# Another split of a second layer between two ways of computing its experts, a longer pause behind each scatter, and a new order of the instruction streams

## The chip, the cores and the metric

The kernel runs on one core of one Trainium2 chip. The metric is the device time of one execution in microseconds. Before the change the median of three runs is 879.16 us (878.42 to 881.28).

## The reference

Two layers over x of shape (8, 512, 128): causal attention and a mixture of experts, then an RWKV block and the same mixture of experts again, each with a layer norm ahead of it and a residual. The mixture has 32 experts; each token goes to its best four, with at most 4·4096·4/32 = 2048 pairs for an expert, and a shared expert is added.

```python
x = L0_attn_a_embeddings                                  # (8, 512, 128)
x = x + attention(_layernorm(x), W_Q, W_K, W_V)
x = x + _L0_ffn_ref(_layernorm(x), Wg, W1, W2, W3, Ws1, Ws2, Ws3)
x = x + rwkv(_layernorm(x), ...)
x = x + _L0_ffn_ref(_layernorm(x), Wg, W1, W2, W3, Ws1, Ws2, Ws3)
# _L0_ffn_ref, over the tokens xf (4096, 128):
scores = jax.nn.softmax(xf @ Wg, axis=-1)
weights, indices = jax.lax.top_k(scores, TOP_K)           # TOP_K = 4
...
for e in range(E):                                        # E = 32, H = 64
    pos = jnp.nonzero(pair_expert == e, size=C, fill_value=P)[0]
    ...
    out = swiglu(xf[tok], W1[e], W2[e], W3[e]) * w[:, None]
    y = y.at[tok].add(out)
z = swiglu(xf, Ws1, Ws2, Ws3)
return (y + z).reshape(B, S, D)
```

## The kernel before

A sequence is a block of 512 tokens by 128 channels, kept in SBUF in a tile `res` of its own through both layers; everything is float32. Eight sequences, numbered 0 to 7, pass both layers.

The mixture of experts can be computed in two ways, and a table, `RUNS`, says for each layer which sequences take which.

- *By all experts* (`FULL`): `full_up` multiplies the whole sequence with the first matrices of two experts at a time (16 pairs, line 706: two matmuls of 128x512 for each), forms the gated hidden values (lines 709 to 714, one activation and three VectorE operations of 128x512), and `full_down` adds the second matrices' products up in PSUM (line 676, four matmuls of 128x128 for each pair). The gates come from `gates`, which writes them to HBM; `full_up` loads them back spread over the partitions (line 695, tile `g`, two buffers).
- *Through pages* (`PAGED`): two or three neighbouring sequences form a group. `route` works out for every token and each of its four experts a row in a paged table in HBM. `scatter` (line 505) writes the normalized tokens there by 16 indirect DMAs for a sequence, issued by POOL, with a pause behind each: a clear of a small tile, `idle` (line 307), that nobody reads. `experts` goes through the group's pages, four pages of 128 rows to a unit: a load (tile `xg`), then stages turned (transposes, L345 and L563), up (L575 to L589), down (L596, L601) and give (L608, L614), and a store to `ys`. `combine` (line 656) adds the results to `res` by 16 indirect gathers with addition, again issued by POOL. A group of n sequences has `pages_of(n)` pages, which is n·512·4/128 + 31, made up to a multiple of four.

Before the change layer 1 has sequences 0 and 7 by all experts and the groups 1 to 3 and 4 to 6; layer 2 has the groups 0 to 2 and 3 to 5, and sequences 6 and 7 by all experts. A group of three has 80 pages, so 20 units.

The order is written out by hand, or by a program outside of the file. The work is split into streams, Python generators that emit a few instructions and yield. The string `ORDER` names a stream by two characters for each step, and `play` steps the streams in that order. On each engine the instructions then stand in exactly that order and are executed in it, each waiting for what it needs; so an instruction that waits holds up all behind it on its engine. SP issues the plain loads and stores in the same way. The streams' letters are: `a` attention and routing of layer 1, `s` scatter, `x` shared expert, `d` and `e` the two halves of a sequence by all experts, `k l m n` the four stages of a group's units, `u` combine; `r` the RWKV block and the routing of layer 2, and `t`, `y`, `D`, `E`, `K L M N`, `v` for layer 2 what `s`, `x`, `d`, `e`, `k l m n`, `u` are for layer 1. The digit is the sequence, or the group for k to n.

Two things on POOL beside scatters and gathers matter: the inverse roots of the norms (lines 334 and 819) are computed there, and they stand in the same queue. Two PSUM buffers of two banks (`ps2`) are shared by the up stage of the pages and by `full_up`.

Of the kernel before, what the change touches and what calls it, by code (L numbers as in the profile page):

```python
# [79 lines left out]


ORDER = (
    "a1a2a2a0a1a2a2a1a0a3z0a2a1a0a6a3z0a1a2a3a4a2a1a0a1a6a6a4a0a2a2a5a1z0a1a2a2a0a4a5a1a1a2a5a2a1a1a2"
    "a0a3a1a3a2a7a2a1a2a1a2a1a1a0a2a7a2a3a1a1a6a2a0a1a3a2a7a2a1a2a1a2a1a0a2a2a3a1a2a4a0a1a1a3a2a1a2a0"
    "a2a0a2a1a0a0a2a2a3a1a5a2a0a3a2a2a1a1a0a2a3a2a1a7a2a1a2a0a3a6a6a2a1a6a2a6a0a2a0a3a6a0a1a2a0a2a1a2"
    "a1a1a3a6a1a0a3a1a0a3a6a0a6a3a0a0a1a0a6a1a1a3a3a6a3a0a1a3a1a0a1a0a0a6a1a1a3a6a3a3a6a6a0a0a3a6a3a0"
    "a6a0a3a0a3a6a0a3a0a3a6a0a3a0a6a4a6a6a4a0a3a3a6a6a0a0a3a4a6a3a0a6a0a3a0a3a0a3a0a4a6a4a6a0a3a4a3a6"
    "a0a0a3a2a1a0a3a2a3a3a1a1a2a3a1a3a2a4a4a4a2a1a3a5a5a5a1a5a2s1a5a5a5a7a5a5a7a0a2a7a2a7a0a3s2a0x2a6"
    "x2a3a4x2a4a5x2a3a3d0a5a6s2a4d0a4x2d0x2a3a4x2a5a5x0s2a3a6a5x0a3a6l0l0a4l0a6a5a4a6a5d0a6s3a6d0a6d0"
    "x3a4x3a4a5a4a5x3a6a4a5d0a4a5s3a5x3a6a4d0a5x3d0x0a4d0a5x3s3a4x0x3a5a4d0a5x0a4a5a4x0a5s3a4x0a4a4a5"  # L90
    "a4a7a4a5a5a7a4a5s2a7a4a4a5a6a4a5a4x1e0a5a6a7a5a6a4x1a4s1a6x1a5a7a4e0a5x1e0d0a7e0d0a7a4a4a5a4x1s1"
    "d0a4a5a4d0a7x1a7a4d0x1s1d0a4a4d0a7e0a4e0a6d0d0a4d0k0a6a5e0a5a4x4a5a5d0s4x4d0a5d0k0a5e0k0k0l0k0d0"
    "a5s4l0l0l0l0a5m0a5e0m0d0l0l0l0d0s4m0a5m0k0k0k0l0k0d0n0a5s4d0n0l0l0a5l0d0x5e0x5d0m0m0l0x5s5d0l0l0"
    "l0d0k0d0e0k0k0m0k0l0m0x4x5l0l0a7n0s5l0l0n0k0x5x5k0l0l0l0m0x5a6m0s5k0l0a6a6k0m0n0x4l0l0l0n0e0m0k0"
    "a6s5l0k0m0n0a7n0m0n0l0l0x4d0l0a6n0d0k0a6m0k0n0l1s6m0d0l1l0n0n0l0l0l0l0n0k0l0l0l1m0k0l0e0m0n0s6k0"
    "a7l0n0k0m0a7l0n0l0l0x4m0n0k0l0x4k0s6m0l0l0n0l0m0a7x6n0k0a7l0x6k0x6m0l0l0n0l0m0a7s6l0n0a7k0l0l0m0"
    "l0n0k0m0a7k0n0l0a7k0m0n0a7l0l0a7l0m0x6l0n0a7x6k0l0l0m0l0n0k0m0a7n0k0a7l0k0k0l0l0m0l0n0k0m0a7l0n0"
    "a7k0l0l0m0l0n0k0m0x6k1n0a7l0x6m0l0l0n0l0m0a7l0n0a7k1l0l0m0l0n0k1m0a7n0k1a7l1k1a7m0n0m0l1l1d0a7l1"
    "n0d0k1m1d0k1n0l1n0m1a7e0l1l1l1l1a7k1m1l1n1m1u2a7k1d0l1l1d0n1n1d0a7m1k1m1a7k1l1n1d0l1l1l1a7d0k1u2"
    "m1d0k1n1m1e0n1l1a7d0d0l1l1d0n1e0n1u2l1l1e0k1l1l1m1l1k1m1k1m1a7e0m1r0k1l1a7a7n1l1l1r0l1l1a7n1k1m1"  # L100
    "r0u2r0l1n1a7a7m1r0r0r0k1l1l1u1n1a7k1r0m1r0k1r2m1l1r0r0r0l1l1d7l1k1m1r0r0l1m1r2r0d7l1r0r0u1k1r0n1"
    "r2r0r0x7l1r2r0r0r2r0d7r0u1n1n1n1n1x7r0n1r0r0l1r0k1m1r2d7u1m1r2k1r0l1r2r2l1l1x7l1l1r2r2m1k1m1l1r2"
    "r0k1l1r0u3r0l1l1k1m1l1r0r1m1n1k1d7l1r0l1r2x7r0d7m1r0n1m1r1r2k1r2l1r0d7u3k1r0r2d7r0l1r1r2r0l1l1r1"
    "n1k1m1x7r0r0k1r1r1x7u3r0r0r1r0r2r0r1r2r2r2d7u3r2n1m1r2x7l1r0r0l1l1l1r2m1r0k1r1r0k1n1r1r0r1r1r3n1"
    "m1l1r1r0r1r3r0n1l1r2e7r0l1e7r0l1r0r1n1n1r0m1k1n1r0n1m1k1k1l1r1r0r1n1k1l1l1l1r1k1r0n1m1r0r1e7m1l1"
    "n1r0n1k1n1r0l1r1l1r0y0y0l1t0m1r1m1n1r1l1r1n1l1l1l1t0m1r1m1n1r1l1n1l1l1l1t0m1r1m1r1r3r3r2r2d7r1t0"
    "d7r2r1d7r3e7r3r2n1r3n1d7r1r3r3r2r1r1y0r2d7u4r3r3r1r2r3r1r2r1r1r3d7r3e7r1r2d7r1u4r3d7r1r1r2r3r2d7"
# [5 lines left out]
    "r4r3d7r4r5r6e7r4r5r4r3t1y2y2r4r4r3r6r6r6y2y2r5r3r6e7r5t1r5r7r3r5r3r5r3r6r6y2r5r5r6r7r3r5r6r7t1r7"
    "r5r3r3r6r5r4r3r6r5r4r4r3r7K0r4r5r5r5r5K0K0K0K0L0r3r4r4y3r5t3L0r5r6L0L0y3r6y3r6r6M0K0M0t4L0r5K0N0"
    "r6L0r7y3N0r5y3L0L0r6r6M0K0t4r5L0M0r5N0K0y3N0L0r6L0L0L0y3r7t4L0L0L0M0K0r7r6r7M0r6K0N0r7r6M0N0K0t4"
    "L0M0K0r6N0y4N0L0L0L0L0y4K0M0L0L0L0M0N0K0r5r6M0N0K0t3L0M0r5r7N0K0L0L0y4r6N0L0r5K0M0L0M0N0K0t3L0L0"
    "r5N0L0L0r5K0r6M0L0K0r5r6M0r7L0L0r5N0r6r7L0N0r5t3M0K0M0y4K0N0L0L0r6r7r5r6L0N0y4M0L0M0N0r5r5r7K0N0"
    "r6K0y4L0L0L0r7L0y4r5M0K0M0N0K0N0L0L0L0L0r5K0M0L0L0L0M0N0K0r5M0N0L0L1t5M0r6r7L1N0L1L0L0K0r6r6N0K0"
    "L0r7L0r6M0L0L0K0L0t5M0r6N0K0r6M0L0N0K0L0M0r6N0L0L0K0L0N0t5r6M0L0K0r6M0N0L0L0K0K0N0L0K0M0L0L0K0L0"
    "y5M0N0t5K0L0r6N0M0L0r6M0N0L0L0L0r6r6N0L0L0L0r7y5K1r7M0r6r6M0r7r7N0r7r6M0N0K1M0r6N0K1L1N0r6r7K1K1"  # L120
    "L1L1r6L1L1r6K1M1L1v0r7r6M1L1N1K1L1L1N1r6K1M1L1L1L1K1r6M1K1M1r6r7L1K1M1N1L1L1r6v0r7N1L1L1r7N1L1L1"
    "M1L1N1K1M1M1K1r6r7M1v0y5L1r6r6N1L1L1L1K1r6N1N1K1L1N1r6M1L1L1K1L1r6M1N1K1L1r6v0N1M1L1L1K1L1y6M1N1"
    "K1L1y6N1y6M1L1L1K1L1y6M1D6N1K1M1y6L1N1M1r7K1L1L1N1L1v2K1L1N1M1r7L1L1K1L1y6M1K1r7M1L1v0N1M1L1K1L1"
    "D6L1N1v2K1N1y6D6M1N1K1D6r7M1y5K1L1r7y5N1L1L1r7D6N1L1D6r7v2D6M1K1r7L1M1N1K1L1L1L1L1N1r7L1L1L1M1K1"
    "M1y5v2K1r7L1y5M1L1L1N1L1M1K1N1N1K1M1L1M1N1N1L1L1L1K1N1D6v1K1D6M1K1D6M1r7v2K1L1r7N1L1L1K1L1L1N1K1"
    "r7L1L1L1M1v1r7r7E6M1M1N1M1L1N1N1r7L1D6L1L1N1r7v1M1r7r7M1N1r7r7v1E6N1E6D6E6D6D6D6D6D6D6r7E6D6D6v4"
    "D6v1D6D6E6r7r7E6E6r7D6D6r7v4r7r7D6r7D6E6D6D6D6D6D6D6v4r7D6D6r7r7r7r7E6E6D6D6D6D6v4r7D6D6r7y7E6y7"
# [15 lines left out]
def kernel(ctx: ExitStack, tc: tile.TileContext, x, small, vecs, w13, w2, out):  # L143
    nc = tc.nc
# [158 lines left out]
    idle = const.tile([P, PAUSE], F32, tag="idle", name="idle")  # L303

    def pause():

        nc.gpsimd.memset(idle, 0.0)  # L307
# [190 lines left out]
    def scatter(f, b):  # L498

        _, xn, _, rows = routed[f][b]  # L500
        _, lo, _, g = run_of(f, b)
        key = f"scatter{f}_{g}"
        for j in range(NJ):
            for k in range(TOPK):
                i = nc.gpsimd.indirect_dma_start(  # L505
                    out=xs[g][:, :],
                    out_offset=bass.IndirectOffsetOnAxis(ap=rows[:, j, k : k + 1], axis=0),
                    in_=xn[:, j, :],
                    in_offset=None,
                    bounds_check=DUMP + P - 1,  # L510
                    oob_is_err=False,
                )
# [504 lines left out]
```

## Time and profile before

| | us |
|---|---|
| median of the timed runs | 879.16 |
| profiled execution | 944.87 |
| span of the profiled execution | 943.2 |
| scatters on POOL, 192, one | 1.004 |
| clears on POOL, 192, one | 0.279 |
| gathers on POOL, 192, one | 1.612 |
| first and last scatter of layer 1 | 99.3 and 271.4 |
| gathers of layer 1 | 315 to 563 |
| gathers of layer 2 | 747 to 938 |

The profile is of one execution, and its span is longer than the timed runs. An engine's busy time is the time in which at least one of its instructions was under way. Rows of groups name line, engine, operation, what is written and read, and the count; then busy time in us and mean duration in ns of one; then the idle time of the engine just ahead of them. A matmul of float32 appears as two records. For POOL's indirect DMAs the slice is POOL's own part.

### The profile page before, as it was taken

What the parts mean: (1) busy time and instruction counts of PE and PEld (TensorE: products, weight loads), DVE (VectorE), ACT (ScalarE), POOL (GpSimd) and SP (SyncE); (2) the same over time, 40 slices, a digit from 0 to 9 for tenths busy, and PEclk for the clock granted to TensorE, in tenths of its full rate; (3) what the DMA queues carried; (4) which work ended last, traced back from release to release, by engine and by line L of the source; (5) the groups of instructions that cost most, each with busy time, mean ns of one, the idle gap of its engine ahead of it and who ended that gap; (6) DMA issues with size and microseconds to landing.
All of it is one profiled execution on the core that took longest, in us unless ns stands there. A gap on an engine that the chain in (4) does not pass through costs nothing.

```text
span 943.2 us, 14326 instructions
## 1 busy us (share of the span) xinstructions
PE 783.6 (83%) x4096; PEld 550.8 (58%) x4096; DVE 588.5 (62%) x2008; ACT 475.0 (50%) x1130; POOL 615.3 (65%) x682
## 2 busy tenths in 40 slices
PE   4878678958869987896999978887996999999953
...
POOL 6100676768350588864888888968534387888776
PEclk9989979979979999998999979788997999999987
...
GB/s 279 242 220 129 99 68 35 127 104 100 133 92 155 140 136 154 85 78 87 95 34 74 34 34 43 34 89 111 141 130 85 134 176 243 158 108 120 142 86 53
DMA packets 159275, 108.15 MB, mean 115 GB/s; under 512 B 18144, under 2 KB 147552, under 8 KB 158944
## 3 DMA queue, kind: packets, MB, share of 16 engines
...
## 4 chain that ended last, share of the span: by engine, by line
POOL 26%; PE 19%; issue 17%; DVE 4%; ACT 3%; DMA 1%; another core or an unknown queue 1%; POOLq 1%; DVEq 0%; ACTq 0%
POOL res L656 21%; PE o L608 4%; PE acl L575 3%; POOL xs L505 3%; PE turn_x L345 2%; PE ac L706 1%; PE kk L929 1%; POOL rstd_p L819 1%; PE acl L596 1%; PE kv L938 1%; DMA xg<-xs 1%; POOL idle L307 1%; PE s L524 1%; DVE h L586 1%
## 5 line engine op out<-in xcount | busy, mean ns | idle before, releaser
L656 POOL DMA_INDIRECT res<-ys,rows x192 | 309.4, 1612 | 75.7 <-issue 53.3
L505 POOL DMA_INDIRECT xs<-xn,rows x192 | 192.8, 1004 | 104.5 <-issue 38.4
L706 PE MATMUL ac<-fT,pair 128*128 128x512 f32 x256 | 124.8, 617 | 17.2 <-DVE g L713 9.6
L608 PE MATMUL o<-w2s,hz 128*128 x640 | 93.4, 290 | 16.0 <-ACT hz L601 7.5
L575 PE MATMUL acl<-w13s,xgTs 128*128 x640 | 95.3, 295 | 12.4 <-issue 5.6
L608 PEld LDWEIGHTS o<-w2s,hz 128*128 128x128 f32 x640 | 84.2, 201 | 30.0 <-issue 11.4
L575 PEld LDWEIGHTS acl<-w13s,xgTs 128*128 128x128 f32 x640 | 86.0, 206 | 24.5 <-issue 13.0
L334 POOL TENSOR_TENSOR rstd_f<-rstd_f,nhalf 128x4 f32<-128x4 f32 x16 | 19.4, 1213 | 121.3 <-DVE rstd_f L332 59.1
L709 ACT ACTIVATE fh<-ac 128x512 f32<-128x512 f32 x64 | 38.1, 596 | 103.8 <-PE ac L706 69.2
L706 PEld LDWEIGHTS ac<-fT,pair 128*128 128x128 f32 x256 | 47.1, 198 | 62.2 <-issue 39.5
L676 PEld LDWEIGHTS fsum<-w2s,fh 128*128 128x128 f32 x512 | 64.1, 195 | 16.8 <-issue 12.8
L601 ACT COPY hz<-acl 64x256 f32<-64x256 f32 x160 | 58.4, 365 | 28.2 <-PE acl L596 17.3
L676 PE MATMUL fsum<-w2s,fh 128*128 128x128 f32 x512 | 65.9, 278 | 2.1 <-DVE fh L714 2.1
L586 DVE SCALAR_TENSOR_TENSOR h<-h,acl 128x256 f32<-128x256 f32 x80 | 33.6, 420 | 53.0 <-ACT h L583 44.3
L712 DVE SCALAR_TENSOR_TENSOR fh<-fh,ac 128x512 f32<-128x512 f32 x64 | 43.8, 684 | 35.0 <-ACT fh L709 34.1
L614 ACT COPY oc<-o 128x512 f32<-128x512 f32 x80 | 46.7, 585 | 37.0 <-issue 13.3
L580 DVE TENSOR_TENSOR wt<-acl,xg 128x4 f32<-128x4 f32 x80 | 12.8, 160 | 80.7 <-PE acl L575 36.9
L563 ACT COPY xgTs<-turn_x 128x512 f32<-128x512 f32 x80 | 46.8, 585 | 24.5 <-PE turn_x L345 10.4
L345 PE MATMUL turn_x<-ident,xg 128*128 128x128 f32 x320 | 51.6, 287 | 5.8 <-ACT xgTs L563 2.7
L583 ACT ACTIVATE h<-acl 128x256 f32<-128x256 f32 x80 | 30.7, 384 | 47.1 <-DVE wt L580 35.5
L307 POOL MEMSET idle<- 128x192 f32 x192 | 53.5, 279 | 0.1
L713 DVE TENSOR_TENSOR g<-g,ac 128x512 f32<-128x512 f32 x64 | 43.5, 680 | 10.1 <-DMA g<-gd 10.1
...
## 6 DMA issues: line engine op xcount, KB each, us to landing
...
xs<-xn,rows POOLq DMA_INDIRECT x192
res<-ys,rows POOLq DMA_INDIRECT x192
...
```

The source lines that it names most:

```text
L307: nc.gpsimd.memset(idle, 0.0)
L345: nc.tensor.transpose(p[:, j * P : (j + 1) * P], src[:, j, :P], ident)
L505: i = nc.gpsimd.indirect_dma_start(out=xs[g][:, :], out_offset=bass.IndirectOffsetOnAxis(ap=rows[:, j, k : k + 1], axis=0), in_=xn[:, j, : ...
L563: nc.scalar.copy(xT, p)
L575: nc.tensor.matmul(acl[:, j, :EW], xT[:, j * P : (j + 1) * P], w13f[:, bass.ds(at[j], EW)], start=True, stop=True)
L601: nc.scalar.copy(z[half, i, :].rearrange("p (j c) -> p j c", c=H), hT[half])
L608: nc.tensor.matmul(o[:, j * P : (j + 1) * P], z[:, j % 2, j // 2 * P : (j // 2 + 1) * P], w2h[j % 2][:, bass.ds(at[j], P)], start=True, st ...
L614: nc.scalar.copy(flat(oc), o)
L656: nc.gpsimd.indirect_dma_start(out=xa[:, j, :], out_offset=None, in_=ys[g][:, :], in_offset=bass.IndirectOffsetOnAxis(ap=rows[:, j, k : k ...
L676: nc.tensor.matmul(p[:, j * P : (j + 1) * P], h[:, j * P : (j + 1) * P], w, start=False, stop=stop and j == NJ - 1)
L706: nc.tensor.matmul(ac[:, s, :], pair[:, i, s, :], xT, start=True, stop=True)
L712: nc.vector.scalar_tensor_tensor(h, h, 1.0, ac[:, 0, :], ALU.add, ALU.mult)
```

## The change

Three things. In layer 2, sequence 3 is computed by all experts, and the second group has sequences 4 and 5 alone; the first group stays. The pause behind each scatter, in both layers, is two clears in place of one. `ORDER` is new as a whole: it has the streams of the new split (`D3` and `E3` come, `t3` and `v3` go, the second group's streams are shorter), and all others stand in another order too.

```diff
@@ -34,7 +34,7 @@
 PAGED, FULL = True, False
 RUNS = (
     ((FULL, 0, 1), (PAGED, 1, 4), (PAGED, 4, 7), (FULL, 7, 8),),
-    ((PAGED, 0, 3), (PAGED, 3, 6), (FULL, 6, 8),),
+    ((PAGED, 0, 3), (FULL, 3, 4), (PAGED, 4, 6), (FULL, 6, 8),),
 )
@@ -80,54 +80,54 @@
 ORDER = (
-    "a1a2a2a0a1a2a2a1a0a3z0a2a1a0a6a3z0a1a2a3a4a2a1a0a1a6a6a4a0a2a2a5a1z0a1a2a2a0a4a5a1a1a2a5a2a1a1a2"
...
-    "r4r4r5r5r2r4u6r2r4r5r2r5r2r5r5r3r2r3r4u6r5r4r2d7r4d7r5r2L0r3r4L0r3d7r5r4r4r4r5t2L0r5r5r4d7r4r5r5"
...
-    "D7D7D7D7E7E7D7v5D7E7v3D7D7D7D7D7E7D7D7v5D7D7D7E7E7D7D7D7D7E7D7D7v5D7D7D7E7E7D7D7D7D7E7D7v5E7E7E7"
-    "v5"
+    "a2a0a2a0z0a2a2a2a2a2z0a1a0a6a1a3a0a6a1a2a3a2a0a2a0a7a7a1a3a2a2a2a2a2a0a1a6a7a0a1a5a0a0a0a2a1a2a0"
...
+    "r4t1r4r5r3r4r6r4r7r5r5r5r3L0r5r5r5r5r3r6r5r4r4r4y2r5r5r6y2D3D3t2r5r4r4D3y3y3r4r5y3r4y3r5y3r7r6r7"
+    "r7r6r6r5r6y3r5r5D3D3y3D3D3E3r7r7D3D3t2t2E3E3r6L0t2t4r5D3D3D3D3r6r6r5r5r6r5r6E3E3r5D3D3y4D3D3r6y4"
...
+    "D3r5r5r5D3E3D3r5r5t1t1t1K0r5D3K0K0r6r5D3E3K0D3D3r5t4D3L0L0t4L0E3K0r5r6r5L0K0r6r5M0D3E3M0r5r7r6r6"
...
+    "E6v5D7D7D7E7D7D7D7E7E7D7D7D7D7D7E7D7D7D7E7D7D7D7D7E7E7v5D7D7D7D7E7D7E7D7D7D7E7D7D7D7D7D7E7D7D7E7"
+    "D7D7D7D7D7D7D7E7D7D7D7E7v4E7v4E7E7v4v4v4"
 )
@@ -304,7 +304,8 @@
     def pause():
 
-        nc.gpsimd.memset(idle, 0.0)
+        for _ in range(2):
+            nc.gpsimd.memset(idle, 0.0)
```

The functions that the new streams call, `full_up`, `full_down`, `gates` and `experts`, are unchanged.

More of the change, by code (lines that the diff above doesn't have):

```diff
@@ L82 @@
 ORDER = (
-    "a1a2a2a0a1a2a2a1a0a3z0a2a1a0a6a3z0a1a2a3a4a2a1a0a1a6a6a4a0a2a2a5a1z0a1a2a2a0a4a5a1a1a2a5a2a1a1a2"
[L84 to L107, printed above, removed]
@@ L108 @@
-    "r1r3r3r1d7r3d7r1r1r3r2u4d7r2r1r3r1r2r3r3r3r2e7r2r1u4r1r3r3r2r1r1r3r2r2r3d7d7r2r1r1r2d7u5r3r1r4r1"
-    "r2r2r1d7r4r1r2d7r1r2r3e7u5r4r1e7r4e7y0d7r4r3r1d7r3r4d7y0r2r3e7r1r1u5d7r4r1y0r4r1r3r2r4d7r2r1y1r4"
-    "r4d7u5y1r3d7r4y0y1d7y1r4r3r4r4r2r4r4d7r3u6r4y1r4y1r4r2d7r4r3y1r2r3r3r4r4e7r3r3r2e7r4r3u6r3r4r3r3"
-    "r4r4r5r5r2r4u6r2r4r5r2r5r2r5r5r3r2r3r4u6r5r4r2d7r4d7r5r2L0r3r4L0r3d7r5r4r4r4r5t2L0r5r5r4d7r4r5r5"
-    "d7r4r6t2r4r5d7e7r4r4d7r5d7r4r5r4d7r5t2e7d7r4r4r5r5r5d7r4t2d7r5r4r5r5e7r4r4e7r3y2r5r6y2r4r5t1r5r4"
@@ L113 @@
[L113 to L127, printed above, removed]
@@ L128 @@
-    "y7y7D6D6D6D7v3E6y7y7D6D6D6y7v4E7E6E6D6D6E6v3D7D7D7D7D7E6D7D7E6D7v3D7D7E7E7D7D7E7D7D7v3D7D7D7E7D7"
-    "D7D7D7D7E7E7D7v5D7E7v3D7D7D7D7D7E7D7D7v5D7D7D7E7E7D7D7D7D7E7D7D7v5D7D7D7E7E7D7D7D7D7E7D7v5E7E7E7"
-    "v5"
+    "a2a0a2a0z0a2a2a2a2a2z0a1a0a6a1a3a0a6a1a2a3a2a0a2a0a7a7a1a3a2a2a2a2a2a0a1a6a7a0a1a5a0a0a0a2a1a2a0"
+    "a2a0a2a5a3a0a0a2a3a0a3a5a0a2a1a1a2a4a1a4a0a0a0a2a1a2a0a2a2a2a6a0a3a1a0a1a0a0a2a2a3a2a2a0a0a1a0a2"
+    "a1a2a2a0a1a4a1a0a3a2a0a2a1a1a3a3a3a2a2a1a0a1a0a3a3a5a2a2a1a0z0a1a1a0a6a6a1a0a6a1a3a2a2a0a0a3a3a1"
@@ new lines @@
+    "a0a1a6a5a1a2a2a3a1a1a0a0a3a0a6a6a1a0a0a1a1a3a0a0a0a1a1a1a0a1a5a3a3a0a4a2a1a2a1a3a3a1a0a2a0a0a3a4"
+    "a1a1a2a3a6a1a0a1a3a1a4a1a1a6a5a2a0a1a5a0a0a6a6a1a6a3a6a6a3d0a1a1a4a4a3a7a2a3a7a1a6a6a2a7a1a6a4a4"
+    "a1a6a2a5a5a5a6a5a4a6a6a4a7a7a2a2a3s1a4a3a2a6a3a3d0d0a6a6a5a4a3a3a3s2a6a5a3a4a4a3a6a4a6a6a3a4a4a4"
+    "x2a4a5x2a3s1s1a3a6a5a5x2a4s2a6a6a3a6d0a4d0a3a4a3a5a5a5x2a6a6a6a3a3a5x2a4x0a5a3x0x0a4a4a3a3a5a7a4"
+    "a4a4a5a7a7a5a4a3a3a7a4a4a4a4a5x0x0d0d0d0a3d0a5a7a7a4a4a4x0x0a5a4e0a4a4d0a7a7a5e0a5a7a7e0a5a5a5a5"
@@ new lines @@
+    "d0d0a7a5a3a7s1a7a4a4a6a5a7a5s2s2a5a4e0x1a5a6d0a6a6a5x1a4e0d0a7a4l0x1d0a5a7l0l0a4d0a4a7x2d0x2d0a4"
+    "e0a6d0d0d0d0a7d0a6a6d0a6a7e0a6a7a4a7d0a7e0a7e0s3a4x3a4d0x3a4a7d0d0a6x3d0x3e0a7a4x3a4d0x3a7s3s3s3"
+    "d0x3a6x4a5e0x1a7x4d0d0x1d0d0a7a7x4d0k0x1s4s4a7s4d0x4s4a5x4x1a5a5a5a5a5k0k0k0k0a5l0l0l0l0l0a5l0m0"
+    "l0l0a5m0k0e0m0k0k0n0m0k0n0e0a5a5n0n0l0l0l0l0l0l0l0a6m0m0l0k0a6a6a6a5k0k0m0m0d0l0d0a7a7a6x4x4a6d0"
+    "l0n0n0l0n0l0d0s6e0a7m0d0k0k0n0d0m0k0n0a7l0d0l0l0l0d0a5k0s6n0d0m0m0x5l0l0a7d0x5k0l0a7l0x5x5m0n0m0"
@@ new lines @@
+    "k0d0n0x5k0e0l0d0s6a7l0l0a7l0l0e0l0l0l0k0k0m0m0e0n0l1m0m0k0k0l0a7l0l0l0e0n0l0n0l0l0k0k0s6l0r0m0m0"
+    "n0r0a7n0n0x6l0l0m0k0l0l0m0k0n0n0n0m0a7k0l0m0l0x6r0a7k0l0r0l0k0m0l0s5n0a7a7a7x6l0r0r0l0x6s5m0k0x6"
+    "x6a7l0x6r0s5r0l0l0l0m0m0k0k0r0r0r0l0r0k0r0l0r0r0r0r0r0l0l0n0m0n0n0n0k0r0r0a7n0l0m0k0k0r0m0a7r0k0"
+    "l0m0r0l0n0l0n0n0n0n0l0l0l0l0l1m0m0l0k0s5k0n0l1k0m0m0r0l0l0l0l0n0n0l0l0l0l0k1x7d7x7x7m0x7m0n0m0m0"
+    "n0r0x7n0n0n0k1k1r0k1l1l1r0l1r0l1r0m1d7m1n1r0k1r0d7n1d7d7k1r0r0r0r0l1k1d7r0l1l1u2r0l1r0r0r0m1d7k1"
@@ new lines @@
+    "m1k1d7l1d7d7l1r0l1r0n1r0l1l1k1m1l1l1n1m1k1l1r0r0r0u2r0m1m1l1l1u2l1u2k1k1l1r0k1r0m1r0l1x7k1m1l1r0"
+    "l1l1l1x7u1l1l1l1k1r0n1n1m1n1e7m1k1k1n1n1e7r2m1r0m1d7d7d7k1r0l1r0r0l1l1e7l1n1l1r0e7l1m1l1n1m1k1n1"
+    "d7l1d7r2r2m1r2r0r0m1k1k1l1k1r0r2d7r2r0l1n1r0d7l1l1n1d7r0r0r2k1m1n1m1d7l1n1k1l1l1u1u1l1r2r2r2r2l1"
+    "l1l1k1m1k1n1n1n1m1l1k1m1u1n1m1r2t0r2r2r2r2r2r1l1l1e7n1l1l1n1n1e7k1r2r1y0m1n1t0r2r2k1m1d7e7d7r2r1"
+    "r2y0l1t0n1y0r1r1r1d7l1l1d7r2l1k1d7d7r1n1r1k1m1r1r2m1u3r1l1l1l1l1k1r1r1k1m1r2l1n1r1l1m1k1l1l1l1l1"
@@ new lines @@
+    "n1e7l1e7k1k1l1m1k1r1r2n1m1l1n1y0k1l1m1l1k1n1r1l1m1r1r1l1m1n1k1l1n1l1r2r1l1m1y0r1r1n1r1r1r2m1l1r1"
+    "r1n1r1l1m1n1u3n1n1x5r1x5d7d7l1u3d7u3y0l1r2t0r1y0r1d7d7r1m1m1r3d7e7n1n1d7d7d7d7d7e7r3r3r2d7d7r3d7"
+    "r2r1e7r1r3r3d7e7d7d7d7r3r1r3r2r3r1r3r3r3r2r1e7r3r3u4r3e7r3r2r3r3r3u4r1r3r1r1r1r1r1r1r1r3r3r2r2r1"
+    "r2r3r1r1r3r3u4r3r2d7r2r2d7r2r2r2d7d7u4d7d7r3r3r3r2r4r1r2u6r1r1r1e7r4r1r2r4r3r1r4r3r3r2e7r4r2r2r1"
+    "u5r3r4r4e7r3r1r4r4r2r7r3r1r4r4r1r2r2r4r4r4r4r1r1r4r4r4r4r1r3r3r3r3r3r4r4r4r3r3r3u6r4r3u5u6r3r3r3"
@@ new lines @@
+    "r3r2r3r2r4r2r4r1r3r1r2r2r4r2r4u6r4r4r4r1r3r2r4r4r1r4r3r4r1r1y1y1y1r4y1r3r4y1r3u5r4u5r4r3r2r3r6r2"
+    "r7r4r3r4r2y1r4r7r5r6r4y1r4r4r4r4r2r4r4r7r7r5r2r4r7r5r3r4r5y2y2y2r4y2r3r6r5r7r3r5r4r3r3r4r5r5L0y2"
+    "r4t1r4r5r3r4r6r4r7r5r5r5r3L0r5r5r5r5r3r6r5r4r4r4y2r5r5r6y2D3D3t2r5r4r4D3y3y3r4r5y3r4y3r5y3r7r6r7"
+    "r7r6r6r5r6y3r5r5D3D3y3D3D3E3r7r7D3D3t2t2E3E3r6L0t2t4r5D3D3D3D3r6r6r5r5r6r5r6E3E3r5D3D3y4D3D3r6y4"
+    "y4r5D3D3E3r5D3D3r5r5y4r6y4y4r6r7r6y4r5r5r6r5r5r5D3D3E3D3D3r6r5E3r5r6r5r5r6r7E3r6r6r5r5D3D3D3r7D3"
```

12 lines of the change are left out of this document (added).

## The prediction

> **What bounds the kernel now.** I read the page first (shares and slices), then busy time by stretch, cut at the ends of the expert groups, then POOL's timeline, then the group rows for prices.
>
> ```profile
> PE 783.6 (83%) x4096; PEld 550.8 (58%) x4096; DVE 588.5 (62%) x2008; ACT 475.0 (50%) x1130; POOL 615.3 (65%) x682
> ...
> PE   4878678958869987896999978887996999999953
> ...
> POOL 6100676768350588864888888968534387888776
> PEclk9989979979979999998999979788997999999987
> ```
>
> TensorE is the busiest engine, yet it has 160 us of idle time in 943.2, and nowhere one long hole: no single engine is the bound throughout. The stretches show who is:
>
> ```profile
> 0.00:99.00 99.00, 73.18 (x364) 49.78 (x364) 54.08 (x300) 55.70 (x146) 23.44 (x78) 0.95 0.89 207
> 99.00:186.00 87.00, 70.54 (x328) 45.93 (x329) 55.40 (x237) 31.77 (x78) 66.06 (x103) 0.90 0.34 87
> 186.00:312.00 126.00, 97.75 (x630) 80.30 (x629) 63.36 (x214) 56.62 (x150) 59.05 (x93) 0.89 0.44 118
> 312.00:461.00 149.00, 126.46 (x693) 92.11 (x692) 109.62 (x345) 90.81 (x218) 111.31 (x88) 0.93 0.50 106
> 461.00:625.00 164.00, 145.63 (x549) 83.53 (x548) 123.67 (x416) 89.25 (x183) 135.64 (x124) 0.93 0.29 54
> 625.00:744.00 119.00, 100.53 (x576) 77.34 (x575) 69.70 (x225) 68.66 (x166) 63.93 (x98) 0.90 0.41 111
> 744.00:832.00 88.00, 83.72 (x566) 66.99 (x565) 50.75 (x166) 59.42 (x152) 70.80 (x46) 1.00 0.84 177
> 832.00:943.00 111.00, 85.80 (x403) 54.87 (x401) 61.89 (x112) 22.81 (x42) 85.09 (x54) 0.90 0.58 106
> ```
>
> Columns: window, length, busy PE, PEld, DVE, ACT, POOL, clock, DMA share, GB/s. I call A the first four rows (layer 1, 461 us), B 461 to 625 (from the end of layer 1's experts to the start of layer 2's), C 625 to 744 (layer 2's first group), D 744 to 832 (second group), E the tail. POOL paces B: its gathers and scatters follow each other without a hole:
>
> ```profile
> 561.88 1.56 POOL L656 DMA_INDIRECT res<-ys,rows  x1 [0.30 <-issue]
> 563.74 1.07 POOL L505 DMA_INDIRECT xs<-xn,rows  x1 [0.30 <-issue]
> 564.81 0.27 POOL L307 MEMSET idle<- 128x192 f32 x1
> 565.26 1.48 POOL L505 DMA_INDIRECT xs<-xn,rows  x1 [0.18 <-issue]
> 567.18 0.98 POOL L505 DMA_INDIRECT xs<-xn,rows  x1 [0.17 <-issue]
> ```
>
> A gather comes every 1.86 us (558.14, 560.02, 561.88 in that timeline), an undisturbed scatter every 1.41 us. POOL also ends the kernel: the chain that ended last is gathers from 749 to 938 us, while TensorE's last matmul ends at 929.
>
> ```profile
> L656 POOL DMA_INDIRECT res<-ys,rows x192 | 309.4, 1612 | 75.7 <-issue 53.3
> L505 POOL DMA_INDIRECT xs<-xn,rows x192 | 192.8, 1004 | 104.5 <-issue 38.4
> L706 PE MATMUL ac<-fT,pair 128*128 128x512 f32 x256 | 124.8, 617 | 17.2 <-DVE g L713 9.6
> L676 PE MATMUL fsum<-w2s,fh 128*128 128x128 f32 x512 | 65.9, 278 | 2.1 <-DVE fh L714 2.1
> L307 POOL MEMSET idle<- 128x192 f32 x192 | 53.5, 279 | 0.1
> ```
>
> **What the Trainium skill says.** "TensorE: Matmul & The Clock Gate", part 1 on the clock gate: after about one idle window of 3.4 us the clock is halved. The trace agrees: granted clock 1.00 in D, where PE is 95% busy, 0.89 to 0.90 where it is 78 to 84% busy. So filling PE's holes pays twice. "Perfetto Trace Analysis", section on the software-generated DMA of GPSIMD: POOL's slice is the making of descriptors, not the transfer; a clear behind it therefore adds to POOL's time and cannot overlap it, as the timeline shows. "SBUF — State Buffer", on who interferes with whom: a GpSimd operation and some VectorE operations exclude each other on a shared port. Here no sign of it: L586 takes 421 ns under scatters, 419 under clears and 420 with POOL idle, so a second clear should cost POOL alone.
>
> **The change part by part.** Sequence 3 of layer 2 leaves the pages. The group of three (80 pages, 20 units) becomes a group of two: 2·512·4/128 + 31 = 63, so 64 pages, 16 units. One unit costs PE (95.3 + 93.4 + 51.6 + 32.9)/80 = 3.42 us, DVE 1.58 and ACT 2.48 from the rows of its lines; four units are 13.7, 6.3 and 9.9. A sequence by all experts costs PE (124.8 + 65.9)/4 = 47.7, DVE 131.7/4 = 32.9, ACT 38.1/4 = 9.5. Net: PE +34.0, DVE +26.6, ACT about 0. All PE rows add to 899 us where the engine is busy 783.6, so +34 is some +30 of busy time.
>
> POOL loses 16 gathers (16 × 1.86 = 29.8) and 16 scatters with their clear (16 × 1.45 = 23.2), and gains a clear behind each of 176 (176 × 0.279 = 49.1): −4 in all. But the clears are paid early, in A and B (148 of the 176 scatters stand there) and the gathers are saved in the tail. On SP, 8 page loads and stores go and 8 gate loads, 1 gate store come; with a DMA share of 0.29 in B I cost them at nothing (bounds −2 and +3: what hides them is that idle queue; a load in front of a page load would add its landing).
>
> The new order. I count, from the order of instructions on each engine, what stands between the same landmarks, each at its row's duration. PE rows, before and after: A 418.9 and 437.3, B 159.4 and 198.1, C 118.0 and 119.3, D 106.2 and 104.1, E 96.8 and 76.1. Gathers and scatters on POOL in B: 48 and 32, then 48 and 36; in D and E 48 and 48 gathers before, 48 and 32 after.
>
> A: the first group's 48 scatters take 99.3 to 178.9 us, 67.7 of issue and 12 of waiting for routing (POOL runs in order; behind each wait stand scatters, and behind these the first page load). Second clears add 13.4, of which the 12 of waits can absorb most. The second group's 13.4 hide: it ends at 272, its loads start at 303. PE has 18.4 more in rows, 16 busy, beside 93 idle. Bounds 0 and +22; I take +10, half of the PE work hidden.
>
> B: PE work is 198.1 × 145.6/159.4 = 181 us. POOL: 4 scatters more (6.8), 32 second clears (8.9), two more roots (2.4): 164 + 18 = 182. Both must fit; at D's 95% PE needs 190, at B's own 89% 203. Sequence 3's matmuls stand in this stretch and in C. Bounds 182 and 203; I take 192, +28.
>
> C: same work (101.6 busy against 100.5), better filled, since sequence 3's matmuls spread over it: bounds −12 and +4, I take −2. D: −1.
>
> E: POOL no longer ends it. Its 32 gathers are 59.5, with some 7 left over from D and 5 for the last store 72. PE: 76.1 × 85.8/96.8 = 67.5 busy, at 97% 70, plus the stall which the last sequence has today on its gate load, 9.6 (below), plus 6 for the copy and store: 85, −26. Bounds −32 and −18.
>
> ```profile
> DVE g L713 <- DMA g<-gd: 10.1, 1, 10.1
> ```
>
> Sum: 10 + 28 − 2 − 1 − 26 = +9, a span of 952. The profiled execution took 944.87 us for a span of 943.2; the median of the timed runs is 879.16, 0.932 of that span. 952 × 0.932 = 888.
>
> **The rivals.** *The filler is free.* Sequence 3 fills the trough of 550 to 750 us, where windows of 50 us have PE at 80 to 89% and the slices' clock falls to 0.7, while the tail still shrinks: A 0, B +20, C −10, D 0, E −28, so −18 and 862 us. For it: the shortest stretches of PE idle are spread exactly there, and the clock is won back. Against: B asks PE, DVE and POOL together for over nine tenths. It decides from the point where A, B and C together grow by less than 27 us. *POOL blocks in order.* The new order puts a normalization root of sequence 6 in front of the whole scatter of sequence 3 in layer 1, and one of sequence 5 before the last 12 scatters of the first group in layer 2; if DVE reaches them late, experts start late: A +22, B +39, C +4, E −26, so +39 and 915 us. For it: POOL waited 34.3 us for one such root before (at 273 us, with nothing due behind it); here scatters are due. *It cancels.* A +5, B +22, C −2, D 0, E −26 gives −1, 878. That the change doesn't do what it says is excluded by the order: 352 clears, 176 scatters, 76 units.
>
> **How the numbers follow.** Forecast (slower by about 1%) 0.40, free filler 0.36, blocked POOL 0.15, cancelling 0.09. The forecast's own range is 882 to 900; the other cases lie on both sides, so that for 8 in 10 I go from 860, just below the free filler's sum, to 912, just short of the blocked POOL's. A measurement of this kernel tells about 0.3% from no change: faster 0.36, same 0.09, slower 0.55.
>
> **What would show it.** Right: end of layer 1's experts near 471, layer 2's first page transposes near 663, N-group ends near 780 and 866, PE working until some 6 us before the end and POOL idle before it; clears 352 × 0.28; PE busy near 814. Wrong: layer 2's experts start before 650 (filler free, clock above 0.93), or after 675 with a long POOL wait on a root (blocked). A tail longer than 95 us would mean that the end is not PE's.

## The result and the profile after

| | us |
|---|---|
| kernel after, median of 4 runs | 888.11 (886.71 to 889.83) |
| kernel before, 4 runs beside it | 878.79 (876.61 to 881.28) |
| ratio | 1.0106, 95% interval 1.0071 to 1.0141 |
| profiled execution of after, its span | 886.87, 885.2 |

The change makes the kernel about 1% slower. The first lines of its page, the busy times and the slices:

```profile
PE 778.0 (88%) x4206; PEld 542.3 (61%) x4206; DVE 607.6 (69%) x2017; ACT 471.2 (53%) x1124; POOL 615.0 (69%) x810
...
PE   3999887989978899898798859969999999999993
...
POOL 6214777777774687877888887677736527888776
PEclk9999998979989999999799969989999999999997
```

A slice is 22.1 us. TensorE's row has its weak places where POOL scatters: the fifth to seventh digit (8, 8, 7: 88 to 155 us) beside layer 1's first group, the twentieth to twenty-seventh (down to 5 and 6: 420 to 597 us) beside layer 2's.

The execution from which the prediction was worked out (span 943.2) was not like the timed ones: the kernel before, profiled again as it was (run before_again below), has a span of 875.3, and the extra 68 us stand in A (45) and C (23). From here on this second profile stands for before, unless the first is named. Its stretches, cut at the same landmarks (first scatter, first transposes of the first group's pages, end of the first group, end of the second, then for layer 2 first transposes, end of the first group, end of the second); columns as in the prediction: window, length, busy PE, PEld, DVE, ACT, POOL, clock, DMA share, GB/s:

```profile
0.00:99.00 99.00, 73.19 (x365) 50.19 (x365) 54.58 (x301) 56.14 (x146) 23.69 (x79) 0.95 0.86 207
99.00:178.00 79.00, 68.06 (x328) 43.75 (x329) 54.46 (x234) 31.09 (x77) 66.31 (x102) 0.96 0.37 96
178.00:261.00 83.00, 78.97 (x579) 66.99 (x576) 57.66 (x194) 51.19 (x137) 58.01 (x94) 1.00 0.59 163
261.00:419.00 158.00, 134.57 (x751) 98.71 (x750) 116.04 (x370) 97.17 (x234) 111.85 (x89) 0.95 0.52 112
419.00:581.00 162.00, 143.69 (x544) 82.76 (x543) 122.57 (x413) 88.14 (x182) 135.27 (x123) 0.93 0.29 52
581.00:679.00 98.00, 93.07 (x587) 73.01 (x585) 70.96 (x228) 68.35 (x168) 64.59 (x99) 0.97 0.51 139
679.00:769.00 90.00, 85.97 (x568) 68.37 (x569) 50.48 (x165) 59.03 (x150) 73.05 (x47) 0.98 0.82 172
769.00:875.00 106.00, 83.67 (x388) 53.04 (x386) 60.13 (x109) 22.34 (x41) 81.52 (x52) 0.92 0.60 108
```

The same of the kernel after:

```profile
0.00:77.00 77.00, 60.00 (x328) 40.97 (x329) 48.03 (x274) 51.34 (x136) 23.43 (x78) 1.00 1.08 262
77.00:184.00 107.00, 91.06 (x446) 60.10 (x445) 74.48 (x290) 41.21 (x102) 80.84 (x157) 0.94 0.33 86
184.00:285.00 101.00, 91.19 (x615) 75.28 (x614) 72.69 (x253) 61.87 (x160) 71.55 (x137) 0.94 0.47 125
285.00:420.00 135.00, 121.59 (x710) 88.85 (x708) 93.97 (x283) 79.58 (x193) 102.37 (x87) 0.97 0.65 140
420.00:626.00 206.00, 172.66 (x642) 96.90 (x642) 153.03 (x469) 104.47 (x214) 163.16 (x186) 0.91 0.28 53
626.00:722.00 96.00, 94.58 (x660) 77.88 (x661) 71.70 (x244) 67.64 (x172) 46.16 (x87) 1.00 0.51 137
722.00:806.00 84.00, 82.54 (x525) 63.10 (x525) 47.30 (x140) 49.72 (x124) 68.25 (x44) 1.00 0.84 179
806.00:885.00 79.00, 64.42 (x290) 39.24 (x288) 46.40 (x71) 15.38 (x26) 59.20 (x38) 0.93 0.56 106
```

Layer 1 (the first four rows) is as long as it was. The fifth row, B, is 206 us against 162: the whole loss and more. TensorE gets less done there in each us (172.66 of 206, clock 0.91), while POOL's instructions follow each other there with only 7.8 us of waits over 1 us. The last row shows the gain in the tail, 79 against 106. The group rows of POOL in after, and the scatters' row in before_again:

```profile
L657 POOL DMA_INDIRECT res<-ys,rows x176 | 282.5, 1605 | 86.8 <-issue 49.0
L506 POOL DMA_INDIRECT xs<-xn,rows x176 | 180.8, 1027 | 113.6 <-issue 74.8
...
L308 POOL MEMSET idle<- 128x192 f32 x352 | 94.1, 267 | 10.2
```

```profile
L505 POOL DMA_INDIRECT xs<-xn,rows x192 | 193.7, 1009 | 82.1 <-issue 30.4
```

The clears are 352 × 0.267 us of busy time, near the 0.279 that the prediction took. But the idle time ahead of the scatters that waits for nothing has grown from 30.4 us (38.4 in the first profile) to 74.8, with 16 scatters fewer. The price was not in the clear's own duration alone.

### The profile page after: what moved, and what is told of

Its sections match the earlier page's. It is cut to its first block, busy times and chain, and to the rows that moved or that the text cites. A ratio compares the mean times of both kernels' runs of the same rounds, so it can differ in the third digit from the quotient of the medians.

```text
span 885.2 us, 14583 instructions
## 1 busy us (share of the span) xinstructions
PE 778.0 (88%) x4206; PEld 542.3 (61%) x4206; DVE 607.6 (69%) x2017; ACT 471.2 (53%) x1124; POOL 615.0 (69%) x810
## 4 chain that ended last, share of the span: by engine, by line
POOL 32%; PE 27%; issue 17%; DVE 10%; DMA 7%; ACT 5%; POOLq 1%; SPq 0%; ACTq 0%; DVEq 0%
POOL res L657 18%; POOL xs L506 8%; PE acl L576 4%; POOL idle L308 4%; PE o L609 3%; DMA res<-ys,rows 3%; PE ac L707 3%; DMA xg<-xs 2%; PE turn_x L346 2%; PE fsum L677 2%; PE lg L374 1%; PE acl L597 1%; POOL rstd_f L335 1%; DMA res<-in_x_dram 1%; PE o L783 1%
## 5 line engine op out<-in xcount | busy, mean ns | idle before, releaser
L657 POOL DMA_INDIRECT res<-ys,rows x176 | 282.5, 1605 | 86.8 <-issue 49.0
L506 POOL DMA_INDIRECT xs<-xn,rows x176 | 180.8, 1027 | 113.6 <-issue 74.8
L707 PE MATMUL ac<-fT,pair 128*128 128x512 f32 x320 | 156.8, 616 | 13.6 <-DVE g L714 13.6
L308 POOL MEMSET idle<- 128x192 f32 x352 | 94.1, 267 | 10.2
L677 PEld LDWEIGHTS fsum<-w2s,fh 128*128 128x128 f32 x640 | 80.8, 195 | 22.7 <-DVE fh L715 10.7
L677 PE MATMUL fsum<-w2s,fh 128*128 128x128 f32 x640 | 85.2, 279 | 1.9 <-DVE fh L715 1.4
L713 DVE SCALAR_TENSOR_TENSOR fh<-fh,ac 128x512 f32<-128x512 f32 x80 | 54.6, 682 | 46.7 <-ACT fh L710 46.6
L609 PE MATMUL o<-w2s,hz 128*128 x608 | 80.1, 277 | 0.5 <-ACT hz L602 0.4
L715 DVE TENSOR_TENSOR fh<-fh,g 128x512 f32<-128x512 f32 x80 | 55.4, 692 | 2.8
L346 PEld LDWEIGHTS turn_x<-ident,xg 128*128 128x128 f32 x304 | 36.8, 145 | 14.3 <-DMA xg<-xs 6.1
```

The costliest lines, as they stand in the source:

```text
L346: nc.tensor.transpose(p[:, j * P : (j + 1) * P], src[:, j, :P], ident)
L506: i = nc.gpsimd.indirect_dma_start(out=xs[g][:, :], out_offset=bass.IndirectOffsetOnAxis(ap=rows[:, j, k : k + 1], axis=0), in_=xn[:, j, : ...
L609: nc.tensor.matmul(o[:, j * P : (j + 1) * P], z[:, j % 2, j // 2 * P : (j // 2 + 1) * P], w2h[j % 2][:, bass.ds(at[j], P)], start=True, st ...
L657: nc.gpsimd.indirect_dma_start(out=xa[:, j, :], out_offset=None, in_=ys[g][:, :], in_offset=bass.IndirectOffsetOnAxis(ap=rows[:, j, k : k ...
L677: nc.tensor.matmul(p[:, j * P : (j + 1) * P], h[:, j * P : (j + 1) * P], w, start=False, stop=stop and j == NJ - 1)
L707: nc.tensor.matmul(ac[:, s, :], pair[:, i, s, :], xT, start=True, stop=True)
```

## The experiments

The experiments ran on four chips, numbered 3, 5, 14 and 8. The kernel before took 878 us on chips 3 and 14, 932.5 on chip 5 and 937.9 on chip 8. So times are compared on one chip unless said otherwise. My theory after the result (1): the second clear costs far more than it was priced, and split and order give that back. The rivals: (2) the second clear is cheap and the new order or split costs the time in B; (3) the second clear pays for itself by something that it keeps away. The expectations number their theories anew for each run; what they call theory 4 is a later form of (3).

### Clears alone

These four ran on chip 3.

**before_again**: no edit.

> The kernel before, unchanged, for a second profile: the one read for the prediction has a span of 943 us, the timed runs 879. Theory 1 (uniform): a span of 876 to 881 in which every stage is shorter by the same 6.8%: layer 1's last page output near 429, layer 2's first page transposes near 583, ends of its two groups near 693 and 775, tail 104 us. Theory 2 (in places): single instructions last as long as before, the lost 64 us lie in some stages alone, and the clock is above 0.923.

877.06 us, span 875.3, clock 0.951. Its stretches stand above: the lost time lay in two stages, as the expectation's theory 2 has it.

**before_two_clears**: the change's third part alone, in the old order and split.

```diff
-        nc.gpsimd.memset(idle, 0.0)
+        for _ in range(2):
+            nc.gpsimd.memset(idle, 0.0)
```

> Before with the second clear alone. Theory 1 (clears on POOL's path): 8.9 us of them stand between layer 1's last gathers and layer 2's first page load, 1 to 13 us before layer 1's first page load: 10 to 22 us slower, 889 to 901. Theory 2 (clears lie beside other work): within 3 us of 879.

973.47 us, ratio 1.1071 (1.1044 to 1.1098): the clear alone costs 95 us, over four times the most that either theory had.

**after_one_clear**: the change without it (the same diff backwards, in the kernel after).

> After with one clear. Theory 1: 10 to 22 us faster than after, 866 to 878, so at or below before; the second clear is then the whole loss. Theory 2: within 3 us of 888; split and order are the loss.

836.69 us, ratio 0.9528 (0.9501 to 0.9554). Split and order alone gain 42 us, and the second clear takes 51.4 of 888.1. Both expectations missed this size as well.

**before_no_clear**: the clear in the kernel before is taken away.

```diff
-        nc.gpsimd.memset(idle, 0.0)
+        pass
```

> Before without any clear. Theory 1: the first clear costs what the second does: 10 to 22 us faster, 857 to 869. Theory 2: no change within 3 us. Theory 3 (the pause serves something): slower, and the scatters get longer than 0.97 us or another engine waits.

863.76 us, ratio 0.9819 (0.9789 to 0.9849). The time is inside the first theory's range, but its reason is wrong: the first clear costs 15 us, the second 95, though they are the same instruction. POOL's timeline says why. Columns: start, duration, engine, line, operation; in brackets the idle time before it and what ended it. First the kernel before with no clear, then after_one_clear_b (the kernel after with one clear, profiled again), then after with two:

```profile
105.78 0.97 POOL L505 DMA_INDIRECT xs<-xn,rows  x1 [0.30 <-issue]
107.06 0.97 POOL L505 DMA_INDIRECT xs<-xn,rows  x1 [0.30 <-issue]
```

```profile
102.74 0.97 POOL L505 DMA_INDIRECT xs<-xn,rows  x1 [0.16 <-issue]
103.71 0.27 POOL L307 MEMSET idle<- 128x192 f32 x1
104.15 0.97 POOL L505 DMA_INDIRECT xs<-xn,rows  x1 [0.16 <-issue]
```

```profile
103.66 0.97 POOL L506 DMA_INDIRECT xs<-xn,rows  x1 [0.47 <-issue]
104.62 0.59 POOL L308 MEMSET idle<- 128x192 f32 x2
105.69 0.97 POOL L506 DMA_INDIRECT xs<-xn,rows  x1 [0.47 <-issue]
```

The scatter itself is 0.97 us throughout. From one to the next it is 1.28 us with no clear, 1.41 with one and 2.03 with two, as subtracting the starts shows; the medians over all scatters of these runs are 1.28, 1.42 and 2.04. The first clear sits in a gap that was there anyway (0.30 becomes 0.27 + 0.16). The second adds 0.32 of its own and 0.31 of idle time before the next scatter. So it costs 0.62 us, not 0.279: over 176 scatters 109 us of POOL's time in place of 49.

### Order and split

The next four ran on chip 5, where the kernel before took 932.54 us.

**after_no_clear**: no clear at all in the kernel after.

> After without any clear behind a scatter. A scatter then comes every 1.27 us as in before without clears, not 1.41: 176 x 0.14 = 25 us less on POOL. Theory 1 (POOL's time counts where it paces, about half of it as in before, where 192 x 0.14 = 27 gave 15): 822 to 828. Rival (the pause serves the new order): 837 or more.

907.71 us (902.29 to 924.52), ratio 0.9724 (0.9682 to 0.9766). Its scatters come every 1.28 us as expected, but both forecasts of the time were set for a chip on which before takes 878 us, so the number decides for neither.

**after_two_in_layer1**: the second clear behind layer 1's scatters only.

```diff
-    def pause():
+    def pause(f):
-        for _ in range(2):
+        for _ in range(2 if f == 0 else 1):
...
-                pause()
+                pause(f)
```

> After, but the second clear behind layer 1's 96 scatters alone. Theory 1 (each stage pays its own clears: 28 us in layer 1, 23 between the layers): layer 1's last page output near 417 as in after, layer 2's first transposes 187 us behind it as with one clear, 862 to 868 in all. Rival (what layer 1 loses is made up later, since POOL then runs ahead of nothing): 837 to 850.

869.51 us, ratio 0.9322 (0.929 to 0.9355), with landmarks near those of theory 1 (layer 1's last page at 414.5, layer 2's first transposes 189 us later). On this chip two clears in layer 1 and one in layer 2 are better than none at all, the opposite of what chip 3 lets one expect. It is taken up below under the third theory.

**before_split**: the old order with the new split, one clear. The steps of `t3`, `v3` and of the last four units are taken out of `ORDER`; those of `D3` are set one by one behind steps of `r3` and others in B and C, each `E3` a few steps later.

```diff
-    "r5r3r3r6r5r4r3r6r5r4r4r3r7K0r4r5r5r5r5K0K0K0K0L0r3r4r4y3r5t3L0r5r6L0L0y3r6y3r6r6M0K0M0t4L0r5K0N0"
...
+    "r5r3r3r6r5r4r3r6r5r4r4r3r7K0r4r5r5r5r5K0K0K0K0L0r3r3r4r4D3D3y3r5L0D3r5r6L0D3L0y3r6y3r6r6M0K0M0t4"
```

> Before with the new split alone, one clear: the steps of sequence 3 by all experts put into before's order one by one after its routing, the streams of its scatter and gathers and of four units taken out. Theory 1 (the split shortens the tail and lengthens the stretch between the layers; the order of layer 1 is the other gain): layer 1's last page output near 416 as before, tail some 82 in place of 108, 860 to 875. Rival (the split is the whole gain): 835 to 850. Second rival (the order is all): 879 or more.

954.64 us, ratio 1.0254 (1.0221 to 1.0287). Its first group of layer 2 is stretched to 151 us (619 to 770); that my places for sequence 3's steps hold that group up is likely, but was not shown. It shows that the split, put into the old order in this way, gains nothing, and no more.

**after_unsplit**: the other way round, the new order with the old split and one clear. `D3` and `E3` go, `t3` and `v3` come back behind `t1` and `v5`, four units' steps are doubled.

```diff
-    "r4t1r4r5r3r4r6r4r7r5r5r5r3L0r5r5r5r5r3r6r5r4r4r4y2r5r5r6y2D3D3t2r5r4r4D3y3y3r4r5y3r4y3r5y3r7r6r7"
...
+    "r4t1r4r5r3r4r6r4r7r5r5r5r3L0r5r5r5r5r6r5r4r4r4y2r5r5r6y2t2r5r4r4y3y3r4r5y3r4y3r5y3r7r6r7r7r6r6r5"
```

> After's order with before's split, one clear: the steps of sequence 3 by all experts taken out, its scatter, gathers and four units of pages put back. Theory 1: first scatter near 76, layer 1's last page output near 389 as in after with one clear, tail as long as before's 108: 845 to 860. Rival (split is the whole gain): 875 to 885. Second rival (order is all): 835 to 842.

930.05 us, ratio 0.9998 (0.9974 to 1.0023). It can't be set beside the numbers of chip 3, so it was run again on chip 14, where before took 877.9, with two others:

**after_again** and **after_one_clear_b**: after, and after with one clear, a second time.

> After, unchanged, beside the next two. Theory 1 (POOL's time alone): 1.01 times the kernel before wherever that runs in about 878 us. Theory 4 (in the executions where before takes 930 to 943 us, waits of several microseconds that nothing in the profile ends stand on PE, DVE and ACT beside the scatters, and the second clear keeps them away): if before takes about 932 here, after stays within 5 us of 888 and its profile has under 20 us of such waits, against 114 in the first profile of before.

> After with one clear again. Theory 1: 836 to 840, 0.953 of before. Theory 4, if before takes about 932 here: the waits come back beside the scatters, and it takes 865 to 900; if before takes about 878: 836 to 840.

887.93 us (ratio 1.0114, 1.0046 to 1.0182) and 839.02 us (0.9537, 0.9474 to 0.96). The 49 us between them repeat the 51 of chip 3. Before took 877.9 here, so theory 4 was not put to the test.

**after_unsplit_b**: after_unsplit a second time.

> After's order with before's split, one clear, again. Theory 1 (split and order gain in different stages, tail 26 us, layer 1 27 us): 845 to 860 if before takes about 878, that is 10 to 25 us above after with one clear. Rival (the split is the whole gain): as long as before. Second rival (order is all): as long as after with one clear.

894.31 us, ratio 1.0157 (1.0086 to 1.0229): 55 us above after_one_clear_b, and longer than any of the three expectations. Not all of this is the split's. Putting `t3` back left a hole that the real order need not have, seen in POOL's timeline: the scatter behind it starts at 557.44, just after VectorE has written the last of a sequence's rows and gates (553.3 to 556.7):

```profile
534.36 0.99 POOL L505 DMA_INDIRECT xs<-xn,rows  x1 [0.17 <-issue]
535.35 0.27 POOL L307 MEMSET idle<- 128x192 f32 x1
557.44 1.17 POOL L505 DMA_INDIRECT xs<-xn,rows  x1 [21.82 <-issue]
```

Without these 22 us it would be some 872, an estimate, so that the split would be worth about 33 us. What is free of the hole is the tail: its window of 785 to 893 us is 108 us long, as in before, against 82 in after_one_clear.

The stages side by side, from the landmarks of each profile (A to the end of the second group in layer 1, B to the first transposed page of layer 2 (its copy, L563), C and D to the ends of its groups, E the rest), in us:

| | A | B | C | D | E | span |
|---|---|---|---|---|---|---|
| before_again | 416 | 165 | 96 | 90 | 108 | 875.3 |
| before_two_clears | 465 | 191 | 119 | 88 | 111 | 974.5 |
| before_split (chip 5) | 455 | 164 | 151 | 75 | 104 | 948.9 |
| after_unsplit_b (B holds the hole) | 389 | 206 | 92 | 98 | 108 | 893.0 |
| after_one_clear | 389 | 187 | 92 | 85 | 82 | 835.0 |
| after | 417 | 210 | 93 | 84 | 81 | 885.2 |

Read downwards: A's gain of 27 is there with either split, so it is the order's. The tail's 26 is not there without the split; nor does the split bring it in the old order (before_split, 104, where the second group is 15 shorter instead): there POOL's last gather starts at 929 us, but TensorE works until 944, 5 us before the end. So the two are not wholly separable. The second clear costs 28 in A, 23 in B and nothing later. In the old order it also cost 23 in C, where 48 scatters stood; the new one has 27 there, and they are hidden behind TensorE, which is busy 94.58 of 96 us. The first five stretches of after_one_clear_b, to be set against the first five of after and of before_again above:

```profile
0.00:77.00 77.00, 60.03 (x328) 41.04 (x329) 48.74 (x274) 51.35 (x136) 23.44 (x78) 1.00 1.10 264
77.00:168.00 91.00, 86.22 (x447) 58.56 (x445) 74.61 (x291) 40.84 (x102) 78.51 (x121) 0.99 0.40 104
168.00:260.00 92.00, 88.47 (x616) 73.49 (x614) 71.94 (x250) 61.05 (x160) 51.09 (x78) 0.98 0.49 135
260.00:391.00 131.00, 119.83 (x708) 87.56 (x706) 95.49 (x288) 79.70 (x193) 102.77 (x79) 0.99 0.67 143
391.00:579.00 188.00, 168.91 (x652) 95.33 (x653) 151.76 (x464) 104.74 (x215) 150.32 (x141) 0.95 0.31 60
...
```

### Is it the clearing or the second instruction?

**after_one_long**: one clear of twice the length, on chip 8.

```diff
-PAUSE = 192
+PAUSE = 384
...
-        for _ in range(2):
-            nc.gpsimd.memset(idle, 0.0)
+        nc.gpsimd.memset(idle, 0.0)
```

> The kernel after with one clear behind each scatter that is as long as its two together (384 elements in a row in place of two of 192). The same number of elements is cleared with one instruction less. If the time spent clearing is what the second clear costs, POOL's cadence from scatter to scatter stays near the 2.03 us of two clears and the time near 888 us. If it is the second instruction, with the gap that comes with it, the cadence is that of one clear, 1.41 us, plus at most the longer clear's own addition of 0.1 to 0.3 us: 1.5 to 1.7 us, and the time 842 to 862 us. Should the time from the scatter to the next be hidden behind the transfer of its descriptors, even the long clear shows nothing: 1.41 us and 837 to 841 us.

```profile
103.26 0.97 POOL L505 DMA_INDIRECT xs<-xn,rows  x1 [0.17 <-issue]
104.22 0.44 POOL L307 MEMSET idle<- 128x384 f32 x1
104.82 0.98 POOL L505 DMA_INDIRECT xs<-xn,rows  x1 [0.16 <-issue]
```

Median cadence 1.58 us, 843.67 us (843.24 to 846.19). The long clear is 0.44 us where two short ones are 0.59, and the gap stays at 0.16 where two make it 0.47. So of the second clear's 0.62 us, 0.16 are the clearing and 0.46 are its being an instruction of its own. The cadence is what shows this. The time lies 44 us under that of after, and inside the second expectation's range, but after was not timed on this chip: it took 888.11 and 887.93 where before takes 878. The ratio measured here, 0.9006 (0.8923 to 0.909), is to a before of 937.91 and doesn't measure the edit.

### What the pause is for

The third theory took its later form from the runs on chip 5. The instructions of the first profile of before last nearly as long as those of before_again (in sum VectorE's, ScalarE's and POOL's differ by 0.1%, TensorE's by 1.7%); what is longer are waits for which the trace names no instruction that ended them (`issue` or `remote`). TensorE's timeline in the first profile of before, while POOL scatters:

```profile
113.61 0.27 PE L775 MATMUL prT<-ident,pr 128*128 128x128 f32 x1
119.17 2.07 PE L524 MATMUL s<-fT,sm 128*128 128x512 f32 x2 [5.29 <-issue]
```

The same place in before_again:

```profile
113.03 0.27 PE L775 MATMUL prT<-ident,pr 128*128 128x128 f32 x1
113.64 1.12 PE L524 MATMUL s<-fT,sm 128*128 128x512 f32 x2 [0.34 <-ACT res L540]
```

In the first profile TensorE, VectorE and ScalarE have 35 such waits of over 1.5 us, 113 us added over the three engines, and 103 of these us lie where POOL scatters, which is under 0.3 of the span. ScalarE and VectorE stand still at the same time as TensorE (5.93 and 5.58 us around 119 us), while POOL's scatters and clears keep their cadence. before_again has two, 3.6 us.

On chip 5 the three lengths of the pause can be compared in layer 1, whose part of `ORDER` is the same in the three kernels:

| layer 1 on chip 5 | cadence of its scatters | such waits in A | A |
|---|---|---|---|
| after_no_clear | 1.28 | 26, 101 us | 448 |
| after_unsplit (one clear) | 1.41 | 12, 29 us | 416 |
| after_two_in_layer1 | 2.03 | 2, 7 us | 414 |

So on this chip a longer pause goes with fewer of these waits, and this is what the second clear can be good for. Each row is one profile. Against one clear the two gain only 2 us there, less than the spread of these kernels' runs: what they keep away and what they cost nearly cancel. after_one_long, on chip 8 where before took 937.91, has four such waits in A, 10 us, and an A of 394, with a pause shorter by 0.46. Closeness is not enough by itself: before_no_clear, on chip 3, scatters every 1.28 us and has two, 3.6 us. What after and after_one_clear take in all on chips 5 and 8 was not tried, so the size of the benefit for the change itself is open; where after was timed, with before at 878 us, there was next to nothing of this to keep away.

## Why the prediction came out right

That the time came out at 888 against 888.11 is luck. The sum of +9 is made of other terms than those that happened: order and split were taken far too high and the second clears far too low, and the two errors cancel. Forecast, and measured as stage after minus stage before_again, with the runs' parts:

| stage | forecast | measured | order and split | second clears |
|---|---|---|---|---|
| A | +10 | +1 | −27 | +28 |
| B | +28 | +45 | +22 | +23 |
| C | −2 | −3 | −4 | +1 |
| D | −1 | −6 | −5 | −1 |
| E | −26 | −27 | −26 | −1 |
| sum | +9 | +10 | −40 | +50 |

- **The second clears.** This term was mis-sized: 13.4 for each group in A, most of it absorbed or hidden, and 8.9 in B. The 0.279 us of the clear's row was taken for the whole cost; the cadence shows 0.62. The timeline that I showed had a gap of 0.17 behind one clear, and I assumed it would stay. Nor does a clear always add its whole duration: the first adds 0.14. In A some 108 scatters start, 67 us of second clears by the cadence, and 28 reach the end of A. The first group's last scatter starts 25 us later than in after_one_clear (174.7 against 149.9) and its first page load 24, but its first transposes only 16 (182.5 against 166.8), since TensorE has other work until then. The other 12 come while the experts run. There the forecast had the second group's clears hide; but POOL now scatters from 76 to 279 us without a wait of over 1 us, and the second group's first load, at 280.8, waits 2.3 us for the last of these scatters, where with one clear it comes at 255.1 and waits for none. In B it is 41 × 0.62 = 25 for a measured 23.
- **A's order.** The forecast counted 18.4 us more of TensorE's rows in A and took half of them as hidden. With one clear TensorE is busy as long as before (355 us against 352), and its idle time in A falls from 64 us to 34: 9 less ahead of the first scatter, which comes at 76 us in place of 99, 6 less between it and the first transposes, 15 less in the second group's stretch. The first scatter's 23 us are not the gain by themselves: the first transposes come 11 earlier (166.8 against 177.7), and the second group starts when it did (259.5 against 259.8). It ends 27 earlier, because its stretch is 130 us in place of 156.
- **B.** With one clear +22; that was within the bounds (+18 to +39, clears included). TensorE's 168.9 us busy of 188 is 90%, as the 89% end of the range supposed. With the second clear POOL is the bound: its 49 gathers at 1.86, 41 scatters at 2.03 and 15 norm operations (23.5 us together) make 198, and only 7.8 of the 206 us are waits of over 1 us. Forecast was 182 for POOL. The number of scatters, four more, was short as well: nine more start in this stretch.
- **C and D** are as forecast in sign; D gains 5 in place of 1, and after_unsplit_b, without the split, has 98.
- **E** is right in size (−27) and wrong in who ends it. The forecast had POOL idle and TensorE working until 6 us before the end. In fact 37 gathers, not 32, run from 807 to 880 us, one per 1.86 us with 4 us of waits, and then the last store. The last instructions on POOL and on TensorE's side (the row of `out_dram` merges two stores, from the first one's start to the second one's end):

```profile
870.79 1.16 PE L677 MATMUL fsum<-w2s,fh 128*128 128x128 f32 x8 [0.94 <-DVE fh L715]
...
872.65 9.60 SPq L672 DMA_DIRECT2D out_dram<-res  x2
...
878.54 1.55 POOL L657 DMA_INDIRECT res<-ys,rows  x1 [0.30 <-issue]
```

TensorE's branch ends with the first of these stores, issued at 872.65 and landed at 875.23, 10 us before the end of the span at 885.2. The second store, issued at 881.87, waits for POOL's last gathers. So POOL ends the kernel as before. The tail is shorter because fewer gathers are left for it: from the end of the last unit on 38 start in after, and 51 in before_again, and 13 × 1.86 = 24 us. That the forecast's 85 us for TensorE's side came near the measured 81 is luck as well.
- **PE busy near 814** is wrong: 778.0. The forecast set out from 783.6 of the first profile, where before_again has 761.2; and of +30 only +17 came. A matmul row of `full_up` is 616 ns in after and in before_again, 602 ns with one clear, where the clock is 0.976: the filled holes win back clock, as the Trainium skill has it ("TensorE: Matmul & The Clock Gate", part 1 on the clock gate), and the second clears spend part of it again (0.956). The window of 3.4 us that the prediction takes from this page is not shown by any run here.
- **The scale.** A factor of 0.932 spread the first profile's surplus evenly. It stood in A (45 us) and C (23) only; B, D and E were already at the timed runs' length. On a sum of +9 this does no harm. It shows in the landmarks: 471 and 663, scaled 439 and 618, against 417 and 627; the group ends, 727 and 807, against 720 and 804. On that scale the sign for free filler, a start before 650, would be one before 606.
- **The shared port.** L586, by which the prediction excluded it, reads one of its operands from PSUM. An operation with both in SBUF, the last of `full_up` (L715 in after), takes 692 ns beside clears, 695 beside scatters and 691 with POOL idle, so that the conclusion stands for these: no sign that the second clear slows VectorE.
- **The rivals.** *Free filler* asked that A, B and C together grow by less than 27; with one clear they shrink by 9 and the time is 837, below its 862; with two they grow by 43. Its terms for B (+20) and the tail (−28) describe split and order well (+22 and −26), its 0 for A does not (−27), and the clears decide the sum. *Blocked POOL* fell: POOL has no wait of 4 us or more from 77 to 279 us, where the first of its two roots stands, nor from 291 to 650, where the second does.
